# Which PSUM tiles fill the last slots of a decoder layer, and where one column tile is summed

## The chip, the core and the metric

The kernel runs on one core of one Trainium2 chip. The metric is the device time of one execution in microseconds (us). The engines are TensorE (PE in the profile, with PEld for its weight loads), VectorE (DVE), ScalarE (ACT), GpSimd (POOL) and SyncE (SP), which issues most of the DMAs.

## The reference

A decoder layer with three residual blocks over x of shape (2, 512, 1024), all in float32:

```python
x = x + attn(layernorm(x), w_qkv, b_qkv, w_o, b_o)     # 32 heads of 32, 8 K/V heads, RoPE, causal
x = x + xattn(layernorm(x), ctx)                       # quantised matmul with ctx (2, 1024, 1024)
x = x + ffn(layernorm(x), W_org, lora_down, lora_up, lora_keys, Wq)

def xattn(x1, x2):
    q1 = fake_quant(x1)          # (clip(round(x / s + z), 0, 255) - z) * s
    q2 = fake_quant(x2)
    return q1 @ q2               # one (512, 1024) x (1024, 1024) product for each batch

def ffn(x):
    base = x @ W_org.T
    coeffs = softmax((mean(x, axis=1) @ Wq.T) @ lora_keys.T / sqrt(K))
    delta = sum over 8 experts e of coeffs[e] * (x @ lora_down[e]) @ lora_up[e]
    return base + delta
```

For the second block the kernel multiplies the rounded integers and needs, beside the product, the sums of the columns of the quantised context of each batch (the zero point's share).

## The kernel before

The kernel works on two batches (b = 0, 1), each with four row tiles of 128 (t = 0 to 3). The context of a batch is 1024 x 1024, in eight tiles of 128 rows (k = 0 to 7), called context tiles or column tiles here.

**Slots.** The attention runs as a sequence of slots, `for i in range(n_slots + LAG): visit(i)`, with LAG = 4. A slot i below `n_slots` computes scores (four PSUM tiles) and, four slots behind, the weights of slot i - 4: scores again, minus a log term, then an exponential on ACT (L1240) that reads the PSUM tile and writes `pt`. So the last four visits have weights and no scores. Some visits also multiply `pt` by the values (PV, L1267), and the result is copied to `oT` (L448 on ACT or L450 on DVE, whichever the planner has free, in `evacuate`).

**PSUM.** The eight PSUM tiles of 128 x 512 are two sets of four, bank00 to bank03 and bank10 to bank13. In each visit one set, `sets[new]`, takes the scores, and the other, `sets[old]`, the weights; between slots other PE work ("filler") uses the set in `allowed`, through `mm()`. At the end of a visit the sets change places by `filler[0] = new`.

**Filler.** All other work of the layer is a queue of generators that give PE work in small steps: projections, the first block's output product (L1411 with `wo`), the second block's product (L1411 with `q` and `q1T`), transposes (L473), the third block (L1774). `fill(us)` runs steps between two slots. The work of the other engines lies in `lanes`, each a list of hops (an engine and a function), and `dispatch(lead)` puts hops into the engines' instruction lists when a planner, the class `Clocks`, holds them due: the engine is not over a lead ahead of PE's time. `Clocks` has a price for each kind of instruction. The order of instructions on every engine is the one in which this program puts them out; nothing reorders them later.

**The context of the second batch.** `load_ctx(1)` works with two buffers `raw`. For each of the eight tiles there are: a load (SP), on ACT the ramp (L1319, `positive`), on DVE the limit (L1323, `limited`, min and add in place, in float32), on ACT the rounding (L1327, `rounded_by_act`) into the bf16 tile `q`. A further lane, (3, "q2sum"), has POOL add up the tiles in f16 (L1382, `sum_columns`): seven additions, k = 1 to 7. `g_columns(1)` then multiplies the sum by a matrix of ones, `onesh` in f16 (L1390, one matmul of 128x512 for each half), and ACT makes `corr` of it (L1398). For batch 0 there is no such sum; there eight matmuls by `onesb`, ones in bf16, do the same. The two constants exist in both kernels.

**Quantised rows.** `quantize_rows(1, t)`, in four lanes, goes: moments (L456 to L461, the power on POOL), multipliers (L1436 to L1440), ACT's scaling (L1470), DVE's limit (L1473), ACT's rounding (L1477), a DMA transpose that ACT issues (L1510), and after `corr` DVE's correction (L1482, L1483). For batch 0 the row total is made on ACT (L1465).

**The third block.** Its product is done with sums of parts of operands: DVE makes sums of `worg` (L644, `tb`) and of x3T (`S`, L1763 and L644), as it did for `wo` (`to`); PE multiplies them (L1774); the results are added to x (L1795), some of them through an intermediate tile (`morewo`, `morewb`, L1711 on DVE and L1724 on ACT).

`chain_units` lists what each unit of PE work depends on; the column sums ("cs", b) depend on ("q2sum", 1) for the second batch.

Of the kernel before, what the change touches and what calls it, by code (L numbers as in the profile page):

```python
# [16 lines left out]
P = 128  # L17
B, S, D = 2, 512, 1024
NH, NKV, HD = 32, 8, 32
CTX = 1024  # L20
# [91 lines left out]
class Clocks:  # L112
# [45 lines left out]
    def add(self, ins):  # L158
        kind = type(ins).__name__[4:]
        engine = str(ins.engine).split(".")[-1]  # L160
        if not kind or kind in ("RegisterMove", "TileManualSchedule") or not ins.outs:
            return
        turning = kind.startswith("DmaTranspose")
        dma = kind == "DMACopy" or turning
        outs = [p.bass_ap for p in ins.outs if hasattr(p, "bass_ap")]
        ins_ = [p.bass_ap for p in ins.ins if hasattr(p, "bass_ap")]
        if not outs:
            return
        names = [(a.tensor.name, p) for a in outs if a.tensor.name in self.written for p in _parts(a)]
        sources = [(a.tensor.name, _part(a)) for a in ins_ if a.tensor.name in self.written]  # L170
        start = 0.0 if dma else self.at[engine]
        for name, part in sources:
            start = max(start, self.written[name].latest(part, engine) + 0.04)
        for name, part in names:
            start = max(
                start, self.written[name].latest(part, engine), self.read[name].latest(part, engine) + 0.04
            )
            if name in self.before:
                old = self.before.pop(name)
                start = max(start, self.read[old].last() + 0.04, self.written[old].last())  # L180
        n = _free(outs[0])
        done = None
        if dma:
            if turning:
                start = max(start, self.at[engine])
                self.at[engine] = start + 0.1
                end = start + 2.0 + n * 0.0012
            else:
                n_bytes = n * 4 * outs[0].ap[0][1]
                start = max(start, self.at["DMA"])  # L190
                self.at["DMA"] = start + n_bytes / 3.2e5
                end = self.at["DMA"] + 2.2
        elif engine == "PE":
            wide = "float32" in str(ins_[0].dtype)
            passes = 1 if not wide else 2 if ins.is_transpose else 4
            size = tuple(ins.tile_size) if ins.tile_size else (128, 128)
            if size != self.tile_size:
                start = max([start] + self.groups) + 0.2
                self.tile_size = size
            whole = size[0] * size[1] == 16384  # L200
            part = range(4) if whole else [max(ins.tile_position) // 32]
            done = max([start] + [self.groups[i] for i in part]) + max(n * passes / 2400.0, 0.055)
            for i in part:
                self.groups[i] = done
            self.at[engine] = done if whole else start + 0.015
            end = done + 0.2
        else:
            many = max([n] + [_free(a) for a in ins_])
            if kind in self.FIXED:
                us = self.FIXED[kind]  # L210
            elif many <= 16:
                us = self.SMALL
            elif engine == "Activation":
                scaled = len(ins_) > 1 and len(outs) == 1
                us = 0.15 + 0.00084 * many + 0.12 * (len(outs) > 1 or scaled and many > 900)
            elif engine == "Pool":
                us = 0.25 + 0.0008 * many
            elif kind == "CustomDveAnt":
                us = 0.08 + 0.00104 * many
            elif kind == "TensorScalarPtr" and len(ins_) < 2 + 2 and not ins.is_scalar_tensor_tensor:  # L220
                us = 0.12 + 0.00058 * many
            else:
                us = 0.08 + 0.00106 * many
                if kind == "TensorScalarPtr":
                    us += 0.05
                elif kind == "TensorTensor" and self.at["Pool"] > start and not _in_psum(ins_):
                    us += 0.1
            if kind == "TensorTensor" and engine == "Pool" and many <= 16:
                us = 0.45
            self.at[engine] = start + us  # L230
            end = start + us + 0.08
        for name, _ in names + sources:
            self.used[name] = self.seen
        for name, part in names:
            self.written[name].add(part, end, engine)
        for name, part in sources:
            self.read[name].add(part, done or end, engine)
            if name in self.bank_read:
                self.bank_read[name] = self.seen
        self.log(ins, engine, names, start)  # L240
# [6 lines left out]
def kernel(  # L247
# [20 lines left out]
    nc = tc.nc  # L268
# [228 lines left out]
    RESERVE = 0.7  # L497
    lanes = {}
    LEAD = 0.6
    LEADS = {"Activation": 5.0, "Pool": 5.0}  # L500

    class Hop:
# [115 lines left out]
    def fill(us):  # L618

        credit[0] += us  # L620
        while any_may() and (is_open() or credit[0] > UNIT / 2):
            if not step():
                credit[0] = min(credit[0], UNIT)
                break

    def close():
# [660 lines left out]
    def load_ctx(b, bufs, dst, release):  # L1287
# [70 lines left out]
                    Hop("DVE", lambda i=i, f=follow: (rounded(i), f()), tuple, can, **last),  # L1358
                )
        if free[0]:  # L1360
            for k in range(1, CTX // P):
                mine = [("q2", b, i) for i, (n_, _) in enumerate(parts) if n_ in (k - 1, k)]
                last = {"key": ("q2sum", b), "made": lambda: [q2sum[b]]} if k == CTX // P - 1 else {}
                lane(
                    (3, "q2sum"),
                    Hop(
                        "Pool",
                        lambda k=k: sum_columns(b, k),
                        lambda k=k: [q2_of(b, k)],
                        lambda mine=mine: all(key in done for key in mine),  # L1370
                        **last,
                    ),
                )
# [10 lines left out]
    def g_columns(b):  # L1384
        corr[b] = const.tile([P, D], F32, tag="corr", name=f"corr{b}")
        for h in range(2):
            cols = slice(h * 512, (h + 1) * 512)
            ps = mm([P, 512], f"cs{b}_{h}")
            if b in q2sum:
                nc.tensor.matmul(ps, onesh, q2sum[b][:, cols], start=True, stop=True)  # L1390
                yield 0.22
            for k in range(CTX // P if b not in q2sum else 0):
                nc.tensor.matmul(
                    ps, onesb, q2_of(b, k)[:, cols], start=(k == 0), stop=(k == CTX // P - 1)
                )
                yield 0.22
            if free[0]:
                nc.scalar.activation(corr[b][:, cols], ps, AF.Identity, scale=zs[:, 0:1])  # L1398
            else:
                nc.vector.tensor_scalar(corr[b][:, cols], ps, zs[:, 0:1], None, ALU.mult)  # L1400
            yield CLOSED
# [488 lines left out]
    def chain_units(b, w_keys):  # L1890

        turned = [("q", n) for n in range(B * NC)] + [("k", n, h) for n in range(B) for h in range(2)]
        columns = [("q2sum", b)] if b else [("q2", b, i) for i in range(CTX // P)]
        unit(("cs", b), turned + columns, lambda: g_columns(b))
        made["cs", b] = lambda: [corr[b]]
        for t in tiles:
            part = slice(t * P, (t + 1) * P)
            unit(("C", b, t), [("A", b, t), ("cs", b)], lambda t=t: C(b, t))
            unit(("X", b, t), [("x3", b, t)] + w_keys, lambda t=t: g_turn_x(b, t))
            made["X", b, t] = lambda p=part: [x3T[b][:, k, p] for k in range(NK)]  # L1900
# [139 lines left out]
    def visit(i):  # L2040
# [28 lines left out]
        finishing = 2 * pair + j // 2 - 1 if i < n_slots and j in (2, 4) else None  # L2069
        for s in range(4):  # L2070
            if s == 1 and g >= 0:
                empty([(new, 0)])
                pv = take_bank((new, 0))
                attend(g, pv)
            if i < n_slots:
                minimum_and_totals(i, s, sc, finishing)
            if s == 3 and finishing is not None:
                logs = logarithm(finishing)
            next(exponentials)
            if s == 0 and unturned:  # L2080
                turn_terms(unturned.pop())
# [5 lines left out]
            pass  # L2087
        if g >= 0:
            attended_to(g, pv)
        filler[0] = new  # L2090
        last_slots = i + 1 >= n_slots
        allowed[:] = [(1 - new if last_slots else new, s) for s in range(4)]
        dispatch()
        fill(RATE_1 if i < EARLY else RATE_2)
        if finishing is not None:
# [222 lines left out]
```

## Time and profile before

| | |
|---|---|
| median of 3 runs | 656.04 us (655.74 to 656.16) |
| the profiled execution | 655.19 us, its span 653.5 us |
| granted TensorE clock, mean | 0.999 |
| PE busy | 631.9 us (97% of the span) |
| DVE busy | 514.5 us (79%) |
| ACT busy | 299.6 us (46%) |
| POOL busy | 128.8 us (20%) |
| the seven additions of q2sum on POOL | 2.12 to 2.93 us each, from 409.40 to 467.62 |

The profile is one execution. Times in lists are microseconds from the start of the span; a row shows start, length, engine, line (L with the number in the kernel), operation, output<-input, shapes, and a count if several like it follow one another. In square brackets stands the idle time of the engine before the row and what ended it. The chain that ended last is followed back from the last instruction to whatever released each one.

### The profile page before, as it was taken

The numbers are of one execution on the slowest core, as the hardware profiler recorded it, in microseconds if no ns is written. First come the engines' busy times: TensorE is split into PE (matmuls) and PEld (weight loads), VectorE is DVE, ScalarE is ACT, GpSimd is POOL, SyncE is SP. The second block draws the span as 40 slices with busy tenths as digits, with TensorE's granted clock in tenths as the row PEclk, the third lists the DMA queues.
The fourth block names the chain that finished last, engine by engine and source line by source line (L and its number), as shares of the span: only waits on it lengthen the run. The fifth ranks groups of instructions, "written<-read, shape, count | busy, mean of one in ns | idle before, by whom it ended". The sixth has DMA issues, their size and how long they took to land. (4 is left out here: it accounts for less than half of the span.)

```text
span 653.5 us, 9247 instructions
## 1 busy us (share of the span) xinstructions
PE 631.9 (97%) x3190; PEld 301.6 (46%) x3190; DVE 514.5 (79%) x1187; ACT 299.6 (46%) x808; POOL 128.8 (20%) x253
## 2 busy tenths in 40 slices
PE   5998999999999999999999999999999999999997
PEld 5753344444444444444444444444345544444443
DVE  5799889888778988888887689998998544553685
ACT  2145576686655768888897433554101100110100
POOL 2100133233313232333233320440110000000000
PEclk9999999999999999999999999999999999999999
DMA  9930000002021230120101146591000002000105
GB/s 290 335 83 2 9 9 10 10 1 73 10 73 65 73 106 10 46 101 34 33 2 25 25 134 237 169 314 32 1 1 0 33 31 97 1 0 1 65 0 193
DMA packets 42478, 44.64 MB, mean 68 GB/s; under 512 B 19264, under 2 KB 32576, under 8 KB 42432
## 3 DMA queue, kind: packets, MB, share of 16 engines
q1 hardware_dynamic: 24992, 38.82, 17.4%
q10 hardware_dynamic: 17440, 5.25, 4.2%
q8 instruction: 25, 0.41, 0.2%
q14 instruction: 21, 0.17, 0.1%
HBM read 35.66 MB, written 4.19 MB: 61 GB/s over the span
## 5 line engine op out<-in xcount | busy, mean ns | idle before, releaser
L1147 ACT ACTIVATE ms<-ms,stats 128x512 f32<-128x512 f32 (+3 forms) x256 | 141.0, 558 | 70.1 <-DVE stats L1132 70.1
L1132 DVE CUSTOM_DVE_ANT_0 ms<-bank,mask 128x512 f32<-128x512 f32 (+3 forms) x256 | 108.5, 487 | 14.7 <-PE bank L1120 12.9
L1240 ACT ACTIVATE pt<-bank 128x512 f32<-128x512 f32 x160 | 88.0, 590 | 25.3 <-PE bank L1267 9.0
L751 PE MATMUL bank<-xT,wq 128*128 128x512 f32 x192 | 88.0, 600 | 2.7 <-DVE stats L1132 2.7
L1245 POOL TENSOR_SCALAR_AFFINE_SELECT pt<-pt 128x512 f32<-128x512 f32 x64 | 48.9, 782 | 94.5 <-ACT pt L1240 90.3
L1411 PE MATMUL bank<-wo,oT 128*128 128x512 f32 x128 | 59.1, 604 | 0.7 <-ACT pt L1240 0.7
L751 PEld LDWEIGHTS bank<-xT,wq 128*128 128x128 f32 x192 | 34.7, 190 | 41.3 <-issue 35.7
L1218 PE MATMUL bank<-qT,kT 32*128 32x128 f32 (+3 forms) x512 | 49.3, 439 | 1.3 <-DVE x L1420 0.6
L1147 ACT ACTIVATION_READ_ACCUMULATOR ms<-ms,stats 128x1 f32 x256 | 50.1, 196 | 0.0
L1120 PE MATMUL bank<-kT,qT 32*128 32x128 f32 (+3 forms) x512 | 49.0, 461 | 0.0
L1120 PEld LDWEIGHTS bank<-kT,qT 32*128 32x128 f32 x512 | 24.2, 183 | 34.9 <-ACT pt L1240 10.5
L1267 PE MATMUL bank<-pt,v 128*32 128x128 f32 (+3 forms) x512 | 37.8, 435 | 0.0
L1411 PEld LDWEIGHTS bank<-wo,oT 128*128 128x128 f32 x128 | 23.1, 189 | 26.8 <-issue 24.2
L1193 POOL TENSOR_TENSOR stats<-stats,log 128x16 f32<-128x16 f32 x16 | 6.5, 409 | 142.7 <-ACT log L1184 100.3
L1218 PEld LDWEIGHTS bank<-qT,kT 32*128 32x128 f32 x512 | 25.6, 185 | 14.6 <-issue 7.8
L1795 DVE TENSOR_TENSOR x<-x,bank 128x512 f32<-128x512 f32 x36 | 23.1, 680 | 11.1 <-PE bank L1774 5.7
L1411 PE MATMUL bank<-q,q1T 128*128 128x512 bf16 x128 | 28.6, 379 | 1.6 <-ACT pt L1240 1.6
L1267 PEld LDWEIGHTS bank<-pt,v 128*32 128x32 f32 x512 | 16.4, 109 | 27.7 <-issue 24.8
L1774 PE MATMUL bank<-worg,S 128*128 128x512 f32 x64 | 28.3, 592 | 0.0
L1774 PE MATMUL bank<-worg,x3T 128*128 128x512 f32 x64 | 28.0, 594 | 0.0
L1774 PE MATMUL bank<-tb,S 128*128 128x512 f32 x64 | 27.9, 593 | 0.0
L743 DVE TENSOR_TENSOR qT<-bank,qT 128x512 f32<-128x512 f32 x28 | 18.9, 686 | 9.6 <-PE bank L751 9.5
(226 smaller groups left out, 1021.4 us busy)
## 6 DMA issues: line engine op xcount, KB each, us to landing
wq<-in_wqT_dram SPq DMA_DIRECT2D x8, 512.0 KB, 8.5
ctx_raw<-in_ctx_dram SPq DMA_DIRECT2D x8, 512.0 KB, 3.2
wo<-in_woT_dram SPq DMA_DIRECT2D x8, 512.0 KB, 3.1
raw<-in_ctx_dram SPq DMA_DIRECT2D x8, 512.0 KB, 3.9
worg<-in_worgT_dram SPq DMA_DIRECT2D x8, 512.0 KB, 6.2
out_dram<-x SPq DMA_DIRECT2D x16, 256.0 KB, 2.1
x<-in_x_dram SPq DMA_DIRECT2D x7, 512.0 KB, 6.7
x_raw<-in_x_dram SPq DMA_DIRECT2D x4, 512.0 KB, 7.4
```

Source lines behind the costliest of these rows:

```text
L743: nc.vector.tensor_tensor(dst, ps, other, ALU.add)
L751: nc.tensor.matmul(ps[:, part], weight[:, k, :], xs_[:, k, part], start=(k == 0), stop=(k == n - 1),)
L1120: nc.tensor.matmul(sc[s][:, part], qTs[b, c][row(s), t * P : (t + 1) * P], kTs[b][row(s), c // 4, : (t + 1) * P], start=True, stop=True,)
L1132: nc.vector.tensor_tensor_reduce(out=of[s][:, part], in0=sc[s][:, part], in1=mask[:, S - (t + 1) * P :], scale=-scale, scalar=BIG, op0=ALU ...
L1147: nc.scalar.activation(ms[:, part], ms[:, part], AF.Exp, bias=stats[g][:, t, s, 0:1], scale=-1.0, accum_out=stats[g][:, t, s, 1:2],)
L1218: nc.tensor.matmul(sc[s][:, part], kTs[b][row(s), c // 4, kb * P : (kb + 1) * P], qTs[b, c][row(s), kb * P :], start=True, stop=False,)
L1240: nc.scalar.activation(pt[:, s, :], sc[s][:, :n], AF.Exp, scale=scale)
L1245: nc.gpsimd.affine_select(out=diagonal, in_=diagonal, compare_op=ALU.is_ge, fill=0.0, base=0, pattern=[[0, 4], [1, P]], channel_multiplier=-1,
L1267: nc.tensor.matmul(pv[row(s), kb * P :], vs[b][:, kb, h * HD : (h + 1) * HD], pt[:, s, part], start=(kb == 0), stop=(kb == NT - 1),)
L1411: nc.tensor.matmul(ps, l[:, t * P : (t + 1) * P], r[:, cols], start=(k == 0), stop=(k == many - 1))
L1774: nc.tensor.matmul(ps[i], l[:, k, i * P : (i + 1) * P], r(k), start=(k == 0), stop=(k == n - 1))
L1795: nc.vector.tensor_tensor(xh, xh, src, ALU.add)
```

## The change

Five places change.

1. In `Clocks`, the price of a two-operand instruction on POOL becomes 0.1 + 0.0021 us for each element, where it was 0.25 + 0.0008.
2. In `fill`, when no step of PE work can go on, `dispatch` is called once more with a lead of IDLE = 2.5.
3. POOL adds up seven column tiles in six additions. The eighth is multiplied by `onesb` in `g_columns`: for each half a matmul of the sum by `onesh` starts the PSUM tile, and one of the eighth tile by `onesb` is added to it.
4. `chain_units` lets the column sums depend on all rounded tiles and, for batch 1, on the sum.
5. In `visit`, the sets of PSUM tiles no longer change places once the last slot with scores is over: `filler[0]` changes only for i below `n_slots`; after that the filler uses the set `new` and the weights go to the set `old`, the same ones in each of the last four visits; the PV tile comes from `mm()` there.

```diff
             elif engine == "Pool":
-                us = 0.25 + 0.0008 * many
+                us = 0.1 + 0.0021 * many if kind == "TensorTensor" else 0.25 + 0.0008 * many
...
+    IDLE = 2.5
...
             if not step():
                 credit[0] = min(credit[0], UNIT)
+                dispatch(IDLE)
                 break
...
-            for k in range(1, CTX // P):
+            for k in range(1, CTX // P - 1):
...
-                last = {"key": ("q2sum", b), "made": lambda: [q2sum[b]]} if k == CTX // P - 1 else {}
+                last = {"key": ("q2sum", b), "made": lambda: [q2sum[b]]} if k == CTX // P - 2 else {}
...
             if b in q2sum:
-                nc.tensor.matmul(ps, onesh, q2sum[b][:, cols], start=True, stop=True)
+                nc.tensor.matmul(ps, onesh, q2sum[b][:, cols], start=True, stop=False)
+                yield 0.22
+                nc.tensor.matmul(
+                    ps, onesb, q2_of(b, CTX // P - 1)[:, cols], start=False, stop=True
+                )
                 yield 0.22
...
-        columns = [("q2sum", b)] if b else [("q2", b, i) for i in range(CTX // P)]
+        columns = [("q2", b, i) for i in range(CTX // P)] + ([("q2sum", b)] if b else [])
...
             if s == 1 and g >= 0:
-                empty([(new, 0)])
-                pv = take_bank((new, 0))
+                pv = take_bank((new, 0)) if i < n_slots else mm([P, S], f"pv{g}")
                 attend(g, pv)
...
-        filler[0] = new
-        last_slots = i + 1 >= n_slots
-        allowed[:] = [(1 - new if last_slots else new, s) for s in range(4)]
+        if i < n_slots:
+            filler[0] = new
+        allowed[:] = [(1 - new if i + 1 == n_slots else new, s) for s in range(4)]
```

## The prediction

> **What bounds the kernel now.** I read the page first, then what TensorE (PE) waits for, then the chain that ended last, then the lists of single instructions around two places.
>
> ```profile
> PE 631.9 (97%) x3190; PEld 301.6 (46%) x3190; DVE 514.5 (79%) x1187; ACT 299.6 (46%) x808; POOL 128.8 (20%) x253
> ```
>
> PE is busy 97% of the span, so only PE's idle time, or work added to PE, can move the end. The waits of PE after 300 us, with total, count and longest, are few:
>
> ```profile
> PE bank L1411 <- ACT pt L1240: 2.3, 3, 0.9
> PE bank L1390 <- POOL q2sum L1382: 1.3, 1, 1.3
> PE bank L473 <- ACT pt L1240: 0.8, 1, 0.8
> ```
>
> Lines 1 and 3 are the PSUM tiles (the four waits come to 0.71 + 0.89 + 0.67 + 0.80 = 3.07 us), line 2 the column sums: the change has a part for each. PE's list of instructions places the first group, between 358 and 379 us:
>
> ```profile
> 358.01 1.89 PE L1411 MATMUL bank<-q,q1T 128*128 128x512 bf16 x8 [0.71 <-ACT pt L1240]
> 360.79 1.89 PE L1411 MATMUL bank<-q,q1T 128*128 128x512 bf16 x8 [0.89 <-ACT pt L1240]
> 364.64 3.70 PE L1411 MATMUL bank<-wo,oT 128*128 128x512 f32 x8 [0.67 <-ACT pt L1240]
> 378.51 1.14 PE L473 MATMUL bank<-ident,xn_c 128*128 128x128 f32 x8 [0.80 <-ACT pt L1240]
> ```
>
> The chain that ended last runs back from the end over PE alone to 467.67 us, and there it leaves PE, over GpSimd (POOL) and ScalarE (ACT) to VectorE (DVE):
>
> ```profile
> 463.57 0.61 DVE raw L1323
> 464.21 1.16 ACT q L1327
> 465.41 0.09 issue
> 465.50 2.13 POOL q2sum L1382
> 467.63 0.04 issue
> 467.67 0.59 PE bank L1390 x2
> ```
>
> So before 467 us the path is mostly DVE's. Whatever PE wins earlier is given back at 467.67 unless this chain (limit of context tile 7, rounding, POOL's addition, ones matmul) comes earlier too. That is the number to work out.
>
> **PSUM part.** The two instruction lists, side by side, are the same up to 355.93 us on PE, and later in the same order there; only tiles differ. The four waits are on tiles that an exponential (L1240) is still reading; in the changed kernel the products go to the other set, so all 3.07 us go. New is a wait of the next slot's weights (362.60), which now go into tiles whose last exponential ends at 361.71, held on ACT by the DMA transpose of 358.88 (1.21 us): without the waits PE is there about 0.6 us too soon. Net: PE about 2.5 us earlier by 388 us. DVE gets less. One copy of oT moves from DVE to ACT, in front of the row total L1465, which DVE's L1482 at 386.22 waits for; the copy needs the PV product that ends at 385.47, so 385.47 - 2.6 + 0.6 copy + 1.1 total gives DVE at 384.6: 1.6 us earlier. From there to 421 us DVE runs nearly without a gap, so it keeps 1.6.
>
> **Reordered limits, roundings and additions.** With the Pool price of an addition at 0.1 + 0.0021 x 1024 = 2.25 us in the planner (the trace: 2.12) instead of 1.07, and seven additions made six, the lists shift. DVE's limits (L1323, 0.60 each start to start) of tiles 4 and 5 slip one place back; those of 6 and 7 both stand at 463.5. The new call of the planner with IDLE has no cost of its own on the chip; its effect is in these lists. On ACT the rounding of tile 4 comes after the transpose of row tile 0, then the ramp (L1319) of tile 5; the ramp of tile 7 stands behind the last transpose, before the morewb copies. Tile 4's limit gone from its old place: DVE leads by 1.6 + 0.6 = 2.2 us at 429.
>
> Here POOL's additions matter, since they stretch DVE's instructions:
>
> ```profile
> 427.40 1.57 DVE L1440 TENSOR_TENSOR off_b<-off_b,qp_sb 128x1 f32<-128x1 f32 x1
> 434.30 0.68 DVE L1323 TENSOR_SCALAR raw<-raw 128x1024 f32<-128x1024 f32 x1
> 436.15 2.28 DVE L1763 TENSOR_TENSOR S<-x3T 128x1024 f32<-128x1024 f32 x1
> 438.46 1.23 DVE L644 TENSOR_TENSOR S<-S,x3T 128x1024 f32<-128x1024 f32 x1
> ```
>
> and the additions beside them:
>
> ```profile
> 426.83 2.12 POOL L1382 TENSOR_TENSOR q2sum<-q2sum,q 128x1024 f16<-128x1024 f16 x1
> 435.22 2.12 POOL L1382 TENSOR_TENSOR q2sum<-q2sum,q 128x1024 f16<-128x1024 f16 x1 [6.27 <-ACT q L1327]
> 438.83 2.84 POOL L1382 TENSOR_TENSOR q2sum<-q2sum,q 128x1024 f16<-128x1024 f16 x1 [1.49 <-ACT q L1327]
> ```
>
> A 128x1 sum that takes 0.16 elsewhere took 1.57, until the addition was over (428.96); the S sum took 2.28 for 1.23; the addition that began inside an S sum took 2.84, 0.72 more. Each waits for the whole of the other, and who came first runs.
>
> Step a, the limit of tile 5. On ACT (row tile 0 rounded from 430.21 - 2.2, transpose to 430.5, rounding of tile 4 to 431.7) the ramp of tile 5 ends at 432.95. DVE is ready for its limit, in the place of 434.30, at 434.38 - 2.2 = 432.2: 0.75 us lost. POOL meanwhile has tile 4 at 431.75; it starts when DVE's L1473 ends at 432.2, and ends at 434.3. If that holds the limit, DVE loses another 1.35. No row shows a limit held by an addition; the nearest are the 128x1 sum held above (1.41) and, the other way round, the addition at 421.38 that took 2.40 beside a limit. Bounds 0 and 1.35; I take 1.35, since a limit that holds an addition should be held by one.
>
> The Trainium skill ("SBUF — State Buffer", section "SBUF: two separate sides") says that DVE and POOL share one port pair as an exclusive lock for a whole instruction, taken by whichever starts first, on DVE's side by instructions with two SBUF inputs or in a two-port mode. It speaks against this reordering. By that rule a limit (0.68 for 1024 elements, against 1.23 for the S sum) is held as well; by the sum that only two-input instructions are held, the change would end 1.4 to 3.4 us earlier.
>
> Step b, the two S sums. The limit starts at 434.3 as before, so the lead is 0. The rounding of tile 5 ends on ACT at 436.7, in the first S sum (436.2 to 437.4, not stretched this time: +1.05). POOL goes between the two S sums, until 439.45, and the second ends at 440.7 instead of 439.69. DVE is now 1.0 us late.
>
> Step c, to 463 us. tb1_0 (447.26 in the trace) comes 1.0 late, where PE had 1.8 to spare and now is 2.5 early: PE waits 1.7 and keeps 0.8. The ramp of tile 7 in front of the morewb copies costs ACT 1.17 where it cost 0.9 at 445.82: +0.27. DVE's L1795 at 452.75 waits for these copies, so DVE is 1.27 late, and from 452.75 to 463.5 it has no gap to recover in.
>
> Step d, the end of the chain. In the old frame: limit of 6 at 463.50, limit of 7 to 464.78, S sum to 465.91; rounding of 6 ends at 465.36, the addition of tile 6 waits for the S sum and ends at 468.0, where that of tile 7 ended at 467.63. +0.37. So removing the eighth addition does not take an addition off this chain: the seventh stands there now.
>
> Step e, two more matmuls on PE by ones, and two weight loads, with nothing beside them while PE waits: 128x512 bf16 go 0.216 apart (16 in 3.62, the last 0.38 long: 3.24 / 15), so +0.43. Bounds 0.43 and 0.6 with a load uncovered; 0.43.
>
> Sum: 1.27 + 0.37 + 0.43 = +2.07 us. PE's wait at the ones matmul grows from 1.26 to about 3.7. Behind it PE is the bound in both kernels, and what PE waits for shifts with it (the least spare there is 1.6 us, at 490.5). The execution of 655.19 us (span 653.5) becomes 657.25; the median of 656.04 lies 0.85 above that execution, so I predict 658.1 us.
>
> **The rivals.** A measurement of this kernel tells about 0.2% (1.3 us) from no change.
>
> Faster: the limit of tile 5 is not held by POOL's addition. Then DVE leads by 1.4 at 434, the second S sum is done (437.3 - 0.0) as POOL gets the operand at 436.74 and starts after it, and neither loss occurs: the lead is 1.4 + 1.05 = 2.4. At the ones matmul: -2.4 + 0.27 + 0.37 + 0.43 = -1.3, so 654.7. It decides at 0.75 us: if ACT's ramp ends that much sooner, or tile 4's rounding that much later, the limit goes ahead of the addition. For it: such margins are below an instruction's length. Against: the order on ACT is fixed, and both times hang on the same ACT chain.
>
> No change: the limit is held, but POOL does not get between the S sums. The lead is +1.05 instead of -1.0 there: 656.04 + 2.07 - 2.05 = 656.06. The S sums before (438.46 after 438.43) show them following each other, with no addition waiting then, so this is not excluded.
>
> The wait disappears wholly (PE keeps 2.5, and its 1.26 go too): -2.5 - 1.26 + 0.43 = -3.3, 652.7. That needs tile 6 done 2.5 us before PE's place, while its limit stands behind all of the tb sums; nearly excluded.
>
> Slower still: one more addition falls on DVE's run (another 1 to 2 us), 659 to 660.
>
> **How the numbers follow.** Forecast 0.50; no change 0.17; faster as above 0.24 and with the wait gone 0.03; slower still 0.06. Faster by over 0.2% needs 1.3 us, which -1.3 only just reaches, so of its 0.24 some 0.19 lie beyond, 0.05 within. Faster 0.22, same 0.22, slower 0.56. The range, 654.2 to 659.3, holds the forecast, no change, the faster rival with 0.5 us below it, and the nearer end of the slower one. The forecast's own range, with the bounds of steps a to e, is 657.3 to 658.9.
>
> **What would show it.** Right: no waits of L1411 and L473 on L1240 between 358 and 379; a limit near 434 stretched to about 2 us; the second S sum near 438 to 440 stretched to 3.3; PE's wait at L1390's place near 3.7. Wrong at step a: the limit at 0.68 and the addition of tile 4 stretched instead. Wrong at step d: the last addition starting before 465.

## The result, and the profile after

The changed kernel takes 664.28 us (663.49 to 665.66, 4 runs) against 655.96 for the kernel before: a ratio of 1.0123, 95% interval 1.0099 to 1.0146. It is slower, as forecast, but by 8.3 us instead of 2.1, and outside the range. The profiled execution took 663.49 us, its span is 661.7.

First line: busy time of each engine. Then what PE waited for after 300 us (total, times, longest).

```profile
PE 636.3 (96%) x3184; PEld 304.8 (46%) x3192; DVE 515.7 (78%) x1186; ACT 299.9 (45%) x809; POOL 124.6 (19%) x252
```

```profile
PE bank L1417 <- DMA q1T<-a_b: 4.6, 1, 4.6
PE bank L1392 <- POOL q2sum L1384: 3.6, 1, 3.6
```

The four waits on L1240 are gone, as they should be, and the wait at the ones matmul grew from 1.3 to 3.6 (forecast: about 3.7). The first line is the surprise: PE waits 4.6 us for a transposed row tile (`q1T`, written by a DMA transpose), which before had no line at all. And PE is busy 4.4 us longer, of which the added matmuls explain 0.43.

PE's instructions around the new wait:

```profile
376.90 1.09 PE L473 MATMUL bank<-ident,xn_c 128*128 128x128 f32 x8
387.19 1.04 PE L473 MATMUL bank<-ident,xn_c 128*128 128x128 f32 x8
392.86 4.51 PE L1417 MATMUL bank<-q,q1T 128*128 128x512 bf16 x15 [4.63 <-DMA q1T<-a_b]
```

The transposes of 376.90 on PE no longer wait, nor do the products of 358.10 and 363.91. The second row stood at 388.94 before; as the two executions are 0.87 apart at the last common instruction (356.80 against 355.93), PE has won 2.6 us here, as forecast (2.5). Then it loses 4.6, and the next 15 matmuls take 4.51 instead of about 3.4.

What happened to the transfer is seen on ACT and SP, after:

```profile
383.79 0.58 ACT L448 COPY oT<-bank 128x512 f32<-128x512 f32 x1 [4.17 <-PE bank L1269]
383.80 1.25 ACTq L1516 DMA_TRANSPOSE q1T<-a_b  x1
```

```profile
383.90 1.98 SPq L320 DMA_DIRECT2D x<-in_x_dram  x4
```

and before, where the copy was DVE's:

```profile
382.76 1.25 ACTq L1510 DMA_TRANSPOSE q1T<-a_b  x1
```

```profile
385.65 2.06 SPq L320 DMA_DIRECT2D x<-in_x_dram  x4
```

The loads of x (four of 512 KB, into memory that the attention gives back) start when the last PV product ends. Before, the transpose was issued 2.9 us ahead of them; after, 0.1. The list of DMA issues has as its last number the time from the issue to the landing (the end of the transfer), first after, then before:

```profile
q1T<-a_b ACTq DMA_TRANSPOSE x1, 8.6
```

```profile
q1T<-a_b ACTq DMA_TRANSPOSE x1, 3.1
```

A faster PE released the loads 2.6 us sooner (383.90 - 0.87 against 385.65). The transpose, which hangs on DVE and now stands behind a copy on ACT that waits for the same PV product, went 0.2 later (383.80 - 0.87 against 382.76). So nearly all of the lost lead is the loads' earlier start.

The table of windows shows where more of PE's busy time comes from. It has the window and its length, the busy time of PE, PEld, DVE, ACT and POOL, then the granted clock, the DMA share and GB/s.

```profile
393.00:396.00 3.00, 3.00 (x10) 1.15 (x10) 0.32 (x1) 0.47 (x1) 0.00 (x0) 0.65 0.52 201
474.00:478.00 4.00, 3.46 (x7) 1.73 (x8) 2.66 (x4) 1.37 (x2) 0.26 (x1) 0.62 0.01 2
```

After each of the two long waits PE's granted clock is about two thirds in the mean of these windows; in windows of 1 us it is 0.50 for the first 2 us (from 392.8 and from 474.3), then 0.85 and 0.64, then 1.00. By the means, an estimate, 0.35 x 3.0 + 0.38 x 3.46 = 2.4 us of work are lost, in rows that count as busy. About 0.9 more lies at 361.66, where 24 matmuls of the next slot's weights take 2.3 us instead of 1.4 (the wait that the prediction put at 0.6). The other 0.6 of the 4.4 is not assigned.

### The profile page after: what moved, and what is told of

Same layout as the page of the kernel before. It is cut to its first block, busy times and chain, and to the rows that moved or that the text cites. A ratio compares the mean times of both kernels' runs of the same rounds, so it can differ in the third digit from the quotient of the medians.

```text
span 661.7 us, 9238 instructions
## 1 busy us (share of the span) xinstructions
PE 636.3 (96%) x3184; PEld 304.8 (46%) x3192; DVE 515.7 (78%) x1186; ACT 299.9 (45%) x809; POOL 124.6 (19%) x252
## 4 chain that ended last, share of the span: by engine, by line
PE 85%; DVE 8%; issue 2%; DMA 2%; ACT 1%; POOL 1%; ACTq 1%; SPq 0%; DVEq 0%; POOLq 0%
PE bank L753 22%; PE bank L1780 15%; PE bank L1417 12%; PE bank L1863 7%; PE bank L1827 7%; PE bank L1122 6%; PE bank L1269 6%; PE bank L1220 5%; PE bank L473 2%; DMA q1T<-a_b 1%; PE bank L1228 1%; DVE ms L1134 1%; DVE x L1801 1%; DVE S L646 1%; ACTq L1516 1%
```

## Experiments

Two of the five edits do nothing here: with the price of POOL's additions or the dispatch with IDLE taken out of the changed kernel, the built instruction lists of all five engines stay the same. So the change has two parts, the PSUM sets and the column tile. In the code below `...` stands for further lines. The median of the runs of before beside these experiments was 655.9 to 656.2 us.

**The column tile alone.** Of the diff, the edits in `load_ctx`, `g_columns` and `chain_units`.

```diff
-            for k in range(1, CTX // P):
+            for k in range(1, CTX // P - 1):
...
+                nc.tensor.matmul(
+                    ps, onesb, q2_of(b, CTX // P - 1)[:, cols], start=False, stop=True
+                )
```

> Only the column tile part is done: six additions, the eighth tile multiplied by ones; the PSUM sets change places as before. Theory (the lost time is the transfer of the last transposed row tile, which the PSUM part makes late): the order up to the last addition is that of before, PE's wait of 1.26 us at the ones matmul goes, two matmuls cost 0.43, so about 655.2 us, 0.8 us under before. Rival (the reordering of additions and the added matmuls cost the time): above 660 us.

Measured: 654.60 us, ratio 0.9976 (0.9967 to 0.9984). PE at the column sums:

```profile
463.37 3.60 PE L1778 MATMUL bank<-worg,S 128*128 128x512 f32 x8
466.80 0.38 PE L1390 MATMUL bank<-q2sum,onesh 128*128 128x512 f16 x1
467.02 0.38 PE L1392 MATMUL bank<-q,onesb 128*128 128x512 bf16 x1
```

No wait stands in front of the ones matmul. In the order of before the addition of tile 6 was over long ago (440.02 + 2.84), so the eighth tile's was the only one left in the chain, and taking it out does what it says. This part is a gain of 1.3 us (654.60 against 655.91).

**The PSUM sets alone.** Only the edits in `visit`.

```diff
-        filler[0] = new
+        if i < n_slots:
+            filler[0] = new
```

> Only the PSUM part is done; seven additions as before. Theory: PE waits 4 to 5 us for the transposed row tile near 388 us and runs slower after it, as in the changed kernel; the end of the chain has two additions in a row (tiles 6 and 7), so 1.7 us more than the changed kernel: 664 to 667 us. Rival (the column tile part costs the time): within 2 us of before, 654 to 658 us.

Measured: 668.14 us, ratio 1.0178 (1.0164 to 1.0192), just above the expected span. PE's waits:

```profile
PE bank L1390 <- POOL q2sum L1382: 6.1, 1, 6.1
PE bank L1411 <- DMA q1T<-a_b: 5.0, 1, 5.0
```

The transposed tile lands 9.0 us after its issue. Two additions in a row stand in front of the ones matmul:

```profile
473.14 4.91 POOL L1382 TENSOR_TENSOR q2sum<-q2sum,q 128x1024 f16<-128x1024 f16 x2 [22.22 <-ACT q L1327]
```

So the whole loss, and the reordering of limits and additions, comes from the PSUM part; the column part takes 3.9 us off it (668.14 against the changed kernel's 664.28).

**The copy back on DVE.** One instruction of the changed kernel is moved.

```diff
-        evacuate(oT[b][:, c, :], pv)
+        (nc.vector.tensor_copy if by_dve else evacuate)(oT[b][:, c, :], pv)
...
-    attended_to(last - 1, pv)
+    attended_to(last - 1, pv, True)
```

> The changed kernel with one instruction moved: the last oT copy is on DVE, so that on ACT nothing stands ahead of the transpose of the last row tile. Theory A (the copy ahead of the transpose on ACT is what makes it late): issued at about 383.3, it lands in 3 to 4 us, PE waits under 1 us for it, and the time is that of my forecast, about 658 us. Theory B (the loads of x, released by the end of the last PV product at 383.7, take the DMA engines, and 0.6 us ahead of them is too little): PE still waits 3 us or more, and the time stays within 1.5 us of the changed kernel's 664.3.

Measured: 669.41 us, ratio 1.0206 (1.0190 to 1.0221): worse by 5 us than the changed kernel. Neither theory's forecast came. The edit did not bring about what A was to be judged by: on DVE the copy, which waits for the PV product, stands ahead of the rounding that the transpose needs (382.94, the rounding at 383.55), so the transpose is issued at 384.27, not at 383.3, and now 1.2 us behind the loads of x (383.05):

```profile
q1T<-a_b ACTq DMA_TRANSPOSE x1, 11.0
```

```profile
PE bank L1417 <- DMA q1T<-a_b: 8.4, 1, 8.4
```

The wait grows as the transpose falls behind the loads, which speaks for B; whether the copy in front of it on ACT matters by itself, the next run decides, which leaves the copy where it is.

**The loads held until the tile has landed.**

```diff
+    def gate(dst):
...
+        nc.gpsimd.tensor_copy(dst[:, :1], q1T[0][:, NK - 1, S - 1 :])
...
         xi = tail_x([P, D], f"x1_{t}")
+        gate(xi)
         load_x(xi, NT + t)
```

`gate` also stands ahead of the first two loads of `raw`.

> The changed kernel with the loads of x and the first two of raw held back until the transposed row tile has landed (six one-column copies on GpSimd, which is idle there, read that tile and write the first column of each load's target; each load then overwrites it). Theory B (the loads crowd out the transpose): it lands about 3 us after its issue at 383.8 instead of 8.6, PE's wait there falls from 4.6 to under 0.5 us, and 5 to 6 us are won back, unless the later loads make a wait of their own: 658 to 660 us. Rival (the transpose is slow by itself because of where it is issued): the wait stays above 3 us and the time at 663 or more.

Measured: 660.13 us, ratio 1.0066 (1.0053 to 1.0080). The transpose, at 383.59, lands in 3.1 us again and PE has no wait for it, nor a slow clock behind it (1.00 from 386 to 400 us). The copy still stands in front of it on ACT, so the copy is not what makes the landing late; the loads are. They now start 4 us later, and PE meets another wait:

```profile
PE bank L1787 <- DVE tb L651: 5.1, 1, 5.1
```

The next run, which holds the loads less, still has 2.7 of these 5.1 us.

**The loads held only until the row total.** As above, with the copies reading the output of ACT's total of that row tile.

```diff
+        nc.gpsimd.tensor_copy(dst[:, :1], last_total["x"][:, :1])
```

> The changed kernel with the loads of x and the first two of raw held only until ACT has made the total of the last row tile (about 385.5, some 1.7 us after the transpose is issued; held as in the run before this by one-column copies on GpSimd into the loads' targets). Theory (the loads crowd out the transpose, and holding them until it had landed made them late for VectorE): the transpose lands in 3 to 4.5 us, PE waits under 0.5 us for it, no wait of 5 us for the tb sums as with the loads held longer, and the rest of my prediction stands: a limit held by an addition, the second S sum held, PE's wait at the ones matmul about 3.6, 657.5 to 659.5 us. Rival (holding the loads costs as much as the crowding): 660 to 663 us.

Measured: 659.81 us, ratio 1.0054 (1.0035 to 1.0073), 4.5 below the changed kernel and between the two ranges, 0.3 above the theory's and 0.2 below the rival's, so the time alone does not decide between them. The loads start 2.0 us behind the transpose; it lands in 3.0, and PE does not wait for it. Of these kernels it is the nearest to the one that my prediction described, though its loads start 1.9 us later than in the changed kernel (385.79 against 383.90). DVE, and POOL's additions beside it:

```profile
435.96 1.80 DVE L1332 TENSOR_SCALAR raw<-raw 128x1024 f32<-128x1024 f32 x1 [0.73 <-ACT raw L1328]
438.89 1.21 DVE L1779 TENSOR_TENSOR S<-x3T 128x1024 f32<-128x1024 f32 x1
440.13 3.03 DVE L653 TENSOR_TENSOR S<-S,x3T 128x1024 f32<-128x1024 f32 x1
```

```profile
434.94 2.27 POOL L1393 TENSOR_TENSOR q2sum<-q2sum,q 128x1024 f16<-128x1024 f16 x1 [5.14 <-ACT q L1336]
439.76 2.32 POOL L1393 TENSOR_TENSOR q2sum<-q2sum,q 128x1024 f16<-128x1024 f16 x1 [2.54 <-ACT q L1336]
```

The limit and the second S sum are each held until the addition is over, as in steps a and b (the limit ends 0.55 us after its addition, the S sum 1.08 after the other). PE's waits:

```profile
PE bank L1790 <- DVE tb L653: 2.7, 1, 2.7
PE bank L1401 <- POOL q2sum L1393: 2.5, 1, 2.5
```

**Fewer additions.** As the last, and POOL adds up four tiles; four are multiplied by ones.

```diff
-            for k in range(1, CTX // P - 1):
+            for k in range(1, 4):
...
+                for k in range(4, CTX // P):
+                    nc.tensor.matmul(
+                        ps, onesb, q2_of(b, k)[:, cols], start=False, stop=(k == CTX // P - 1)
+                    )
```

> As the run before it, and GpSimd adds up only the first four context tiles; the other four are multiplied by ones (six more matmuls of 0.216 us, 1.3 us of PE). No addition runs beside VectorE after 425 us. Theory (steps a, b and d: additions hold VectorE by the shared lock, and one stands in the last chain): the limit of tile 5 and the second S sum take 0.68 and 1.23 again, 3.1 us less for VectorE, the last addition's 2.1 us leave the chain, PE's wait at the ones matmul falls from 3.6 to under 1.5 us, and the time falls by 1.5 to 3 us against the run before it. Rival (VectorE is late for another reason, such as the late loads): its time stays within 0.7 us of that run, or rises by the 1.3 us of matmuls.

Measured: 656.13 us, 3.7 us under the run before it, more than the 3 us expected; ratio to before 1.0002 (0.9992 to 1.0012).

```profile
435.54 0.69 DVE L1332 TENSOR_SCALAR raw<-raw 128x1024 f32<-128x1024 f32 x1 [0.73 <-ACT raw L1328]
437.35 1.22 DVE L1780 TENSOR_TENSOR S<-x3T 128x1024 f32<-128x1024 f32 x1
438.60 1.23 DVE L653 TENSOR_TENSOR S<-S,x3T 128x1024 f32<-128x1024 f32 x1
```

From the limit's start to the end of the second S sum DVE takes 4.3 us instead of 7.2; PE's waits at the ones matmuls are 1.1 us together, and the wait at the tb sums is gone. That additions hold the limit and the S sum (steps a and b), and that one stands in the last chain, is shown by taking them away. They were taken away together: what each is worth by itself, and the 0.37 us of step d, this run does not tell.

**The transpose first.** The changed kernel, nothing held; DVE rounds the row tile before it normalises the next one, and the last copy is on DVE behind it.

```diff
-                lambda: xn_free[0] > 0,
+                lambda: xn_free[0] > 0 and ((b, t) != (0, 2) or ("a1", 0, 3) in done),
...
-    attended_to(last - 1, pv)
+    attended_to(last - 1, pv, True)
```

> The changed kernel, nothing held, but the last row tile of batch 0 goes first: DVE rounds it before it normalises xn_c 2, and the last oT copy is on DVE, so ACT issues the transpose at about 382.5, some 1.4 us ahead of the loads of x instead of 0.1. Theory (what counts is how far the transpose is ahead of the loads): it lands in 3 to 5.5 us, PE waits under 0.5 us, about 657 to 659.5 us, with the two held instructions of VectorE as before. Rival (1.4 us ahead is too little, since 2.9 was needed): it lands in over 6 us, PE waits 1 to 3 us, 660 to 663 us.

Measured: 654.04 us, ratio 0.9969 (0.9956 to 0.9982), below what I expected. Issued 1.4 us ahead of the loads, the transpose lands in 3.1:

```profile
382.91 1.25 ACTq L1516 DMA_TRANSPOSE q1T<-a_b  x1
```

```profile
384.28 1.97 SPq L320 DMA_DIRECT2D x<-in_x_dram  x4
```

But this edit moves more than it says: the planner also puts ACT's ramp of tile 5 in front of the row tiles, at 426.21, so the limit is ready when DVE comes to it and goes ahead of the addition:

```profile
434.98 0.69 DVE L1325 TENSOR_SCALAR raw<-raw 128x1024 f32<-128x1024 f32 x1
436.78 1.96 DVE L1769 TENSOR_TENSOR S<-x3T 128x1024 f32<-128x1024 f32 x1
438.77 1.22 DVE L646 TENSOR_TENSOR S<-S,x3T 128x1024 f32<-128x1024 f32 x1
```

That is my faster rival (forecast: 654.7) so far as the limit goes; of the S sums the first is still held in part (1.96 for 1.23). How much of the 5.8 us against the kernel with held loads is the order and how much the held loads, this run does not separate.

**Both.** The transpose first, and four tiles added up.

> As the run before it, with only the first four context tiles added up on GpSimd and the other four multiplied by ones. Theory (the two losses are separate and add up): 1.5 to 3.5 us under the run before it, 653.5 to 656 us, no wait for the transpose and under 1.5 us of waits at the ones matmuls. Rival (they share a cause): within 0.7 us of the run before it.

Measured: 653.21 us (652.59 to 653.84), ratio 0.9958 (0.9944 to 0.9972), the fastest of all. Against the run before it that is 0.8 us, between the theory's 1.5 to 3.5 and the rival's 0.7. The order had already taken the held limit away, and what was left to win was PE's wait of 2.4 us at the ones matmul, less 1.3 for six more matmuls. After 300 us PE waits only 0.3 us here, and the ones matmuls follow without a gap:

```profile
460.47 3.60 PE L1781 MATMUL bank<-worg,S 128*128 128x512 f32 x8
463.91 0.38 PE L1392 MATMUL bank<-q2sum,onesh 128*128 128x512 f16 x1
464.12 1.03 PE L1395 MATMUL bank<-q,onesb 128*128 128x512 bf16 x4
```

## Why the prediction was wrong

**The step that failed** is the end of the PSUM part: "Net: PE about 2.5 us earlier by 388 us. DVE gets less." The size was right (2.6), and so was DVE's 1.6 at 386 us (385.46 - 0.87 against 386.22), but I did not ask what PE meets next at 388 us: the landing of the last transposed row tile was left at its old time, and PE's wait for it was put at nothing without a reason. It measured 4.6 us, and 1.1 more for the slow clock behind it. Of the 8.3 us, 4.5 go when the loads are held until the row total (664.28 to 659.81). I noted that the oT copy moves to ACT in front of the row total, and not that the transpose of the same row tile stands behind it too; and I did not count what the earlier PV product releases on SP. Six of the kernels, by how far the transpose is ahead of the loads:

| kernel | ahead of the loads, us | landing, us | PE's wait, us |
|---|---|---|---|
| before | 2.9 | 3.1 | none |
| loads after the total | 2.0 | 3.0 | none |
| transpose first | 1.4 | 3.1 | none |
| changed | 0.1 | 8.6 | 4.6 |
| sets alone | 0.1 | 9.0 | 5.0 |
| copy on DVE | -1.2 | 11.0 | 8.4 |

The four others have leads of 1.4 to 4.5 us and land in 3.0 to 3.1.

The Trainium skill ("DMA: Bandwidth & Descriptors", section "Issuing engines are not separate DMA queues") says that transfers issued by ACT and SP run on the same 16 engines and interleave. The traces agree: before, the transpose's packets (those under 512 B, 1056 of them) move within 2.1 us, from 383.9 to 386; in the changed kernel about as many are spread over 385 to 393 us, while SP's queue moves 2.2 MB in the same time. It is what I should have weighed: a transpose on ACT's queue is not safe from loads on SP's.

**What was left out of the sum.** A slow clock after a long wait was not in it, although I forecast a wait of 3.7 us. It costs about 2.4 us, for two waits. Counted along PE, the sum that would have come out: 2.07, less the wait of 1.7 at the tb sums (PE is late there anyway) and 0.1, plus 4.6 and 2.4, is 7.3 of the measured 8.3. The two profiles are 8.2 apart in span, and 0.87 of that stands already at 356 us, ahead of the change, which leaves 7.3; whether the medians hold a like share, no run shows.

**A wrong attribution.** I put the reordering down to the Pool price and the sixth addition. The built lists show that the price moves nothing, and the list of the sets alone that the PSUM part moves the limits; with six additions and the sets as before, in the column tile alone, the order stays the old one.

**DVE's lead.** I had DVE 1.6 us ahead from 386 to 421, and 2.2 at 429. It had the 1.6 at 386, but in the kernel with the loads after the total it loses them at 402 us (first that kernel, whose execution is 0.88 later at 356 us, then before):

```profile
402.39 1.28 DVE L1811 TENSOR_TENSOR x<-x,bank 128x512 f32<-128x512 f32 x2 [2.11 <-ACT morewo L1740]
```

```profile
401.54 1.29 DVE L1795 TENSOR_TENSOR x<-x,bank 128x512 f32<-128x512 f32 x2
```

The morewo copies stand on ACT behind ramps that wait for the loads of raw. At 429 us the limit in that place starts at 429.74, less 0.88 just where one started before (428.89), so the lead is nil. This was enough to matter: step a needed the lead of 2.2 to end where the kernel before does. Without it the held limit ends 1.9 us later than the limit there before (437.76 - 0.88 against 434.98), and the ones matmul starts 3.2 us later than before (471.71 - 0.88 against 467.67), where steps c and d had 1.64. So without the crowded transfer the change still costs 3.8 us (659.81 against 655.99) and not 2.07, and the missing lead is about the size of the difference. That was read from the trace, not tested, and the holding may have a part in it: in the kernel with the transpose first, where nothing is held, DVE waits 2.22 us at the same place but comes out 0.9 ahead of before (401.90, in an execution that is 1.23 later at 356 us).

**What was right.** The steps that the chain of waits needed are all in the trace of the changed kernel, at a later time: DVE waits 0.77 for the ramp (forecast 0.75), the limit takes 1.76, the second S sum 3.03, the first 1.21.

```profile
438.61 1.76 DVE L1325 TENSOR_SCALAR raw<-raw 128x1024 f32<-128x1024 f32 x1 [0.77 <-ACT raw L1321]
441.49 1.21 DVE L1769 TENSOR_TENSOR S<-x3T 128x1024 f32<-128x1024 f32 x1
442.73 3.03 DVE L646 TENSOR_TENSOR S<-S,x3T 128x1024 f32<-128x1024 f32 x1
```

The last addition does wait for an S sum, and PE's wait is 3.61, forecast 3.7. That this number came so close is luck: in the forecast PE had waited 1.7 at the tb sums and was still 0.8 early, in the changed kernel it came 3.4 late without a wait there, and the chain was 5.8 late instead of 1.6. Where PE does wait at the tb sums (2.7, loads after the total), its wait at the ones matmul is 2.5. In step a the truth lies nearer the upper of the two bounds: the limit, an instruction with one input, is held 1.1 us of the 1.35. That fits the rule of the Trainium skill ("SBUF — State Buffer", section "SBUF: two separate sides") if the limit runs in a two-port mode, which no row shows. Where the transfer is not crowded, the kernels lie at 659.8 with the losses of steps a and b and the loads held, and at 654.0 with nothing held and without the first of them; I had said 658.1 and 654.7.

## What to carry to other kernels

A stall taken from one engine moves every transfer that this engine releases: list the DMAs that start at its next milestones, and ask which small transfer, needed soon, will then share the engines with them. A transpose needs a lead over bulk loads (here 1.4 us was enough and 0.1 was not), not only an issue before its use, and an edit that gives the planner other times can reverse such an order far from the edit. Test the parts of a change alone: here one part gains 1.3 us and the other loses 12.

## What I had not expected of the hardware

A DMA transpose of 128 rows that lands in 3.1 us alone lands 8.6 to 9.0 us after its issue when 2 MB of loads start 0.1 us behind it, and in 3.1 when they start 1.4 us behind it: the effect sets in between these two leads, which was not narrowed down.

PE's granted clock fell to 0.50 for the first 2 us after the waits of 4.6 and 3.6 us in the changed kernel, and for the first 3 us (450.2 to 453.2) after the 2.7 us in the kernel with the loads after the total; after waits of 2.5, 2.4 and 1.3 it stayed at 1.00. Such a wait costs 1.1 to 1.6 us of work beyond itself (estimates, from the clocks in windows of 1 us). The Trainium skill ("TensorE: Matmul & The Clock Gate", section "Why this matters for your kernels") advises no idle gaps above about 3 us; here a gap of 2.7 was already followed by half the clock. Where between 2.5 and 2.7 it sets in, and whether it always does there, was not tested.
